# Tying the last batch's butterflies to their written place on VectorE, in a four-layer convolution chain on one Trainium2 core

## The chip, the cores and the metric

The kernel runs on one core of one Trainium2 chip. The metric is the device time of one execution in microseconds. Smaller is better.

## The reference

An input x of shape (4, 64, 256, 256) in 32-bit floats goes through four layers. Layers 0, 1 and 3 are long convolutions along both image axes, with one separable filter per channel, and a residual term. Layer 2 works in a Haar wavelet domain: a two-dimensional transform, two branches that scale, mix the 64 channels and shrink, and the inverse transform with a residual.

```python
# layers 0, 1, 3: k is an outer product of two generated filters per channel
y = jnp.fft.irfft2(u_f * k_f, s=(fft_size, fft_size))[..., :L, :L]
out = y + x * bias[:, None, None]
# layer 2
f1 = haar2d(x)
for i in range(v.shape[0]):
    f3 = f1 * v[i]
    f4 = jnp.einsum('bchw,oc->bohw', f3, conv_w[i])
    f5 = jnp.sign(f4) * jax.nn.relu(jnp.abs(f4) - tau[i])
    acc = acc + f5
y = haar2d(acc, inverse=True)
return y + x
```

## The kernel before, in words

The separable convolutions are matrix products with Toeplitz matrices. One image (a batch entry and a channel, 256 x 256) needs two products per layer: `first` (tile `pa`, copied by ScalarE to a tile `a`) and `second` (tile `py`, to which VectorE adds the residual in L284). Both call `contract`, L253 and L254. PSUM gives all of them four banks in turn (`psm`).

The work of a batch b has three stages. `convolutions` runs layers 0 and 1 and the forward Haar transform. `mixing` runs 64 groups g of layer 2: channel mix on TensorE into `px` (L441), a scaling split between VectorE (L460) and ScalarE (L465), the absolute value and sign on ScalarE, the shrinking on VectorE (L476, L480), and two additions into the large tile `z` (L486). `inverse` then takes 64 channels c, one for each tick: `fetch` copies a channel out of `z` (`zc`, ScalarE, L525), `rows` transforms the rows on TensorE (`pw`, L532 and L533), `join` adds the layer's residual on VectorE (`t` and `u`, L554, L557, L558), and layer 3's two products (`pa`, `py`) and the output follow. For the last batch, b = 3, the stage `mixing` is accompanied by layer 3 of those images of earlier batches that were put off (`convolution`; their input tile is `v`).

The inverse column transform has two forms. The channels 0 to 15 (chunk 0 of `z`) have it done on TensorE: `halves` (`w`, a ScalarE copy in L539 and a VectorE subtraction in L540) and `cols` (`pu`, L546). The channels 16 to 63 (chunks 1, 2 and 3 of `z`) have it done in place by butterflies on VectorE. `level(n, chunk)` calls `halve`, which issues two VectorE instructions on `z`: a subtraction (L291), and an instruction that makes the sum from it (L292), which needs the first one's result. A chunk has levels n = 1, 2, 4, 8 and 16 in one pair each, n = 32 in two pairs and n = 64 in four: eleven pairs, seven of them with 1024 elements for each partition. All pairs of a chunk have to be done before the first channel of the chunk is fetched.

The order of the work is written as a list of events. Every step has a time in ticks, `at(time, run, unit)`, the list is sorted, and the steps are called in that order. In `inverse`, `when` gives a level its tick; for the last batch these are the tick `start + 16 * (chunk - 1)` for n = 1 to 8, the next one for n = 16, and then every second tick for one pair each of n = 32 and n = 64. That list is not yet the order on the engines: a scheduler orders each engine's instructions anew, and an instruction whose inputs it takes to be ready may be issued far ahead of its place in the list. In the program before, the butterflies of the last batch stand where that scheduler put them: chunk 1's levels 1 to 16, and the first steps of chunks 2 and 3, stand within `mixing`, and the rest is spread over the inverse stage's channels 0 to 31.

Of the kernel before, what the change touches and what calls it, by code (L numbers as in the profile page):

```python
# [16 lines left out]
B, C, S, EMB, ORD = 4, 64, 256, 33, 64  # L17
# [8 lines left out]
PLACE = {  # L26
    "load": 0.714,
    "a0": 1.643,
    "a0 copy": 1.643,
    "y0": 2.571,  # L30
    "y0 sum": 2.571,
    "a1": 3.5,
    "a1 copy": 3.5,
    "y1": 4.429,
# [64 lines left out]
def conv_seq_kernel(ctx, tc, x, fz, fw, bias, decay, haar, haar_row, factors, vt, taut, wmix, out):  # L99
# [14 lines left out]
    nc = tc.nc  # L114
# [126 lines left out]
    def toeplitz(layer, c, name):  # L241

        t = tp.tile([P, 2, S], F32, name=name, tag="toep")
        nc.sync.dma_start(t, ap(pads[layer], c * 2 * ROW, [[1, P], [ROW, 2], [1, S]]))
        return t
# [40 lines left out]

        return [product, residual]

    def halve(even, odd):

        nc.vector.tensor_sub(odd, even, odd)  # L291
        nc.vector.scalar_tensor_tensor(even, even, 2.0, odd, ALU.mult, ALU.subtract)  # L292

    def level(n, chunk, begin=0, count=None):

        count = n if count is None else count
        v = z.rearrange("p n s x c -> p n s (x c)")[:, chunk].rearrange("p (j e s) x -> p j e s x", e=2, s=P // 2 // n)
        halve(v[:, begin : begin + count, 0, 0, :], v[:, begin : begin + count, 1, 0, :])

    def butterfly():  # L300

        v = z.rearrange("p n s (h k) c -> p n s h k c", k=2)
        for h in range(2):
            halve(v[:, :, 0, h, 0, :], v[:, :, 0, h, 1, :])
# [6 lines left out]
    def at(time, run, unit):  # L311
        events.append((time, len(events), run, unit))
# [196 lines left out]
    def inverse(b, start, put_off):  # L509

        st = {}

        def early(c):
            r = mx.tile([P, 2, 2, P], F32, name=f"r_{b}_{c}", tag="f", bufs=3)
            nc.sync.dma_start(r, keep[b][c])
            st[c]["r"] = r

        def sooner(c):
            st[c] = {}
            if c not in put_off:  # L520
                st[c][2] = toeplitz(2, c, f"t2_{b}_{c}")

        def fetch(c):
            a = mx.tile([P, 2, 2, P], F32, name=f"zc_{b}_{c}", tag="mag")
            nc.scalar.copy(a.rearrange("p h k i -> p (h k) i"), z[:, c // 16, :, :, c % 16].rearrange("p i x -> p x i"))  # L525
            st[c]["z"] = a

        def rows(c):
            a = st[c]["z"]
            ps = psm.tile([P, 2, 2, P], F32, name=f"pw_{b}_{c}", tag="mm")  # L530
            for m in range(2):
                nc.tensor.matmul(ps[:, 0, m, :], a[:, 0, m, :], hsinv, start=True, stop=True)  # L532
                nc.tensor.transpose(ps[:, 1, m, :], a[:, 1, m, :], ident)  # L533
            st[c]["pw"] = ps

        def halves(c):
            w = st[c]["w"] = mx.tile([P, 2, 2, 2, P], F32R, name=f"w_{b}_{c}", tag="f4")
            ps = st[c]["pw"]
            nc.scalar.copy(w[:, 0], ps)  # L539
            nc.vector.tensor_tensor(w[:, 1], ps, w[:, 0].bitcast(F32), ALU.subtract)  # L540

        def cols(c):
            ps = psm.tile([P, 2, 2, P], F32, name=f"pu_{b}_{c}", tag="mm")
            flat = "p e m w -> p (e m w)"
            for i in range(2):
                nc.tensor.matmul(  # L546
                    ps.rearrange(flat), hb, st[c]["w"][:, i].rearrange(flat), start=(i == 0), stop=(i == 1)
                )
            st[c]["pw"] = ps

        def join(c):
            ps = st[c]["pw"]
            t = io.tile([P, 2, 2, P], F32, name=f"t_{b}_{c}", tag="res", bufs=BUFS["res"])
            nc.vector.scalar_tensor_tensor(t, st[c]["r"], 0.5, ps, ALU.mult, ALU.add)  # L554
            u = io.tile([P, 2, S], F32, name=f"u_{b}_{c}", tag="y", bufs=BUFS["y"])
            v = u.rearrange("p m (w e) -> p m w e", e=2)
            nc.vector.tensor_add(v[:, :, :, 0], t[:, 0], t[:, 1])  # L557
            nc.vector.tensor_sub(v[:, :, :, 1], t[:, 0], t[:, 1])  # L558
            st[c]["u"] = u

        def aside(c):
            nc.scalar.dma_start(late[b, c], st.pop(c)["u"])

        along = start - groups - 3

        def when(tick, n, chunk, *span):
            at(tick + PLACE["level"], lambda _: level(n, chunk, *span), 0)

        at(along + 11 + PLACE["level"], lambda _: butterfly(), 0)
        for chunk in range(1, 4):  # L570
            turn = start + 16 * (chunk - 1)
            for n in (1, 2, 4, 8):
                when(along + 12 + 3 * chunk if b + 1 < B else turn, n, chunk)
            when(turn + 1, 16, chunk)
            for i in range(2):
                when(turn + 2 + 2 * i, 32, chunk, 16 * i, 16)
            for i in range(4):
                when(turn + 6 + 2 * i, 64, chunk, 16 * i, 16)

        for c in range(C):  # L580
            for name, stage in zip(("sooner", "early", "fetch", "rows"), (sooner, early, fetch, rows)):
                at(start + c + PLACE[name], stage, c)
            turn = start + c
            if c < 16:
                at(start + c + PLACE["halves"], halves, c)
                at(start + c + PLACE["cols"], cols, c)
                turn += 1
            at(turn + PLACE["join"], join, c)
            if c in put_off:
                at(turn + PLACE["aside"], aside, c)  # L590
            else:
                for name, stage in zip(("a3", "a3 copy", "y3", "y3 sum", "out"), last(b, st)):
                    at(turn + PLACE[name], stage, c)

    def last(b, st):
        return [
            *first(b, st, "u", 2, "a3"),
            *second(b, st, "a3", 2, "u", "y3", "co"),
            lambda c: nc.scalar.dma_start(out[b, c].rearrange("(k p) w -> p k w", p=P), st.pop(c)["y3"]),
        ]  # L600
# [41 lines left out]
    start = ready + 3  # L642
    for b in range(B):
# [10 lines left out]
        start = max(end + C, ready + 3)  # L654
# [115 lines left out]
```

## Time and profile before

| | |
|---|---|
| median of 3 runs | 2919.81 us (2915.54 to 2923.6) |
| the profiled execution's own time | 2913.15 us |
| its span | 2911.3 us |
| PE busy in the span | 2827.3 us (97%) |
| DVE (VectorE) busy | 2499.0 us (86%) |
| ACT (ScalarE) busy | 2085.2 us (72%) |
| mean granted TensorE clock | 0.997 |

Times within the execution are microseconds from the start of the span. The last batch's `mixing` lies at about 2386 to 2676, its `inverse` at about 2676 to 2911. Busy time of TensorE is modelled at its ends, so a small gap may hide in it. The names PE, DVE and ACT stand for TensorE, VectorE and ScalarE; SP issues the loads.

### The profile page before, as it was taken

Reading aid. Unit: us, or ns where it says so; the run is one execution under the profiler, and the core shown is the slowest. Engines: PE = TensorE matmul, PEld = TensorE weight load, DVE = VectorE, ACT = ScalarE, POOL = GpSimd, SP = SyncE. Lnnn points to the kernel's source line nnn. Section 1 sums busy time; section 2 is a strip of 40 time slices with the busy share of each in tenths; the row PEclk is TensorE's granted clock in tenths of the full one; section 3 lists DMA queues with packets and bytes.
Section 4 is the critical chain, followed back from the end, with each engine's and each line's share of the span. In section 5 each row is a group of like instructions: output and inputs, shape, how many; then the busy total and the mean of one; then the engine's idle time right before and its main releaser. Section 6 shows DMA issues by size and latency. Waiting matters only on the chain. (4 is left out here: it accounts for less than half of the span.)

```text
span 2911.3 us, 52368 instructions
## 1 busy us (share of the span) xinstructions
PE 2827.3 (97%) x16566; PEld 2551.1 (88%) x16566; DVE 2499.0 (86%) x4263; ACT 2085.2 (72%) x4950; POOL 329.7 (11%) x644
## 2 busy tenths in 40 slices
PE   8999999999999999999999899999999899999999
PEld 6899998888888898998898898998898898887898
DVE  4656558999998679999998679999998779999985
ACT  2333338999995558989985558998986568887554
POOL 0111111121120001221211001121211000000000
PEclk9999999999999999999999999999999999999999
DMA  5878777666676886777677886777777888776676
GB/s 162 256 229 233 231 233 222 205 205 206 197 213 205 268 260 198 214 213 212 208 214 237 253 269 195 214 215 212 208 212 233 262 278 233 235 233 199 208 237 208
DMA packets 599367, 649.77 MB, mean 223 GB/s; under 512 B 48465, under 2 KB 517044, under 8 KB 598964
## 3 DMA queue, kind: packets, MB, share of 16 engines
q1 hardware_dynamic: 519860, 562.09, 65.2%
q10 hardware_dynamic: 79232, 84.34, 8.2%
q8 instruction: 134, 2.20, 0.3%
q14 instruction: 141, 1.16, 0.1%
HBM read 426.77 MB, written 219.48 MB: 222 GB/s over the span
## 5 line engine op out<-in xcount | busy, mean ns | idle before, releaser
L253 PE MATMUL py<-t,a 128*128 128x256 f32 x3072 | 920.9, 382 | 7.5 <-ACT a L267 6.9
L267 ACT COPY a<-pa 128x512 f32<-128x512 f32 x768 | 490.7, 639 | 430.3 <-PE pa L254 390.5
L465 ACT ACTIVATE f<-px,vt 128x64 f32<-128x64 f32 x2816 | 620.2, 408 | 95.9 <-DVE f L460 95.6
L254 PEld LDWEIGHTS py<-t,a 128*128 128x128 f32 x3072 | 584.3, 190 | 79.8
L254 PE MATMUL py<-t,a 128*128 128x128 f32 x3072 | 590.8, 274 | 0.0
L253 PEld LDWEIGHTS py<-t,a 128*128 128x128 f32 x3072 | 496.2, 191 | 47.5 <-ACT a L267 16.8
L441 PE MATMUL px<-wb,f 128*128 128x256 f32 x2048 | 490.4, 381 | 11.1 <-ACT f L465 10.6
L441 PEld LDWEIGHTS px<-wb,f 128*128 128x128 f32 x2048 | 367.7, 190 | 56.4 <-ACT f L465 17.6
L525 ACT COPY zc<-z 128x512 f32<-128x512 f32 x256 | 281.5, 1101 | 170.6 <-PE pw L533 143.6
L343 POOL TENSOR_TENSOR sd<-less 128x128 f32<-128x128 f32 (+4 forms) x320 | 189.3, 592 | 1884.7 <-DVE less L342 1616.8
L469 ACT ACTIVATE mag<-f 128x1024 f32<-128x1024 f32 x256 | 304.1, 1188 | 21.0 <-DVE z L486 20.4
L476 DVE TENSOR_TENSOR mag<-mag,vt 128x1024 f32<-128x1024 f32 x256 | 312.4, 1220 | 4.6 <-ACT mag L469 3.4
L480 DVE SCALAR_TENSOR_TENSOR mag<-mag,f 128x1024 f32<-128x1024 f32 x256 | 312.7, 1222 | 1.1 <-DVE mag L476 0.5
L253 PE MATMUL pa<-t,y 128*128 128x256 f32 x1024 | 308.5, 383 | 4.7 <-DVE y L284 2.9
L253 PE MATMUL pa<-t,x 128*128 128x256 f32 x1024 | 305.7, 380 | 0.0
L366 DVE TENSOR_TENSOR sp<-sd,sp 128x512 fp32r<-128x512 f32 x256 | 179.1, 700 | 135.0 <-ACT sp L361 133.8
L472 ACT ACTIVATE f<-f 128x1024 f32<-128x1024 f32 x256 | 291.4, 1138 | 3.2
L253 PE MATMUL pa<-t,u 128*128 128x256 f32 x772 | 236.0, 388 | 39.2 <-issue 18.9
L284 DVE SCALAR_TENSOR_TENSOR y<-u,bsb,py 128x512 f32<-128x512 f32 x193 | 143.9, 745 | 124.6 <-PE py L254 101.3
L284 DVE SCALAR_TENSOR_TENSOR y<-x,bsb,py 128x512 f32<-128x512 f32 x256 | 189.8, 742 | 42.7 <-PE py L254 41.7
L254 PEld LDWEIGHTS pa<-t,y 128*128 128x128 f32 x1024 | 194.7, 190 | 26.5
L254 PEld LDWEIGHTS pa<-t,x 128*128 128x128 f32 x1024 | 194.6, 190 | 26.3
(72 smaller groups left out, 4450.8 us busy)
## 6 DMA issues: line engine op xcount, KB each, us to landing
t<-pad SPq DMA_DIRECT2D x768, 256.0 KB, 4.0
x<-in_x SPq DMA_DIRECT2D x256, 256.0 KB, 3.8
coef<-co SPq DMA_DIRECT2D x256, 256.0 KB, 3.0
f<-coef SPq DMA_DIRECT2D x256, 256.0 KB, 3.1
r<-keep SPq DMA_DIRECT2D x256, 256.0 KB, 3.7
out_y<-y ACTq DMA_DIRECT2D x256, 256.0 KB, 4.0
keep<-sums SPq DMA_DIRECT2D x256, 128.0 KB, 2.8
keep<-sd SPq DMA_DIRECT2D x256, 128.0 KB, 2.8
```

The costliest lines, as they stand in the source:

```text
L253: nc.tensor.matmul(ps[:, m, :], src[:, 0, m * P : (m + 1) * P], t[:, ::-1], start=True, stop=False)
L254: nc.tensor.matmul(ps[:, m, P:], src[:, 1, m * P : (m + 1) * P], t[:, : P - 1 : -1], start=False, stop=True)
L267: nc.scalar.copy(a, s["p" + new])
L284: nc.vector.scalar_tensor_tensor(y, s[res], bsb[:, layer, c : c + 1], s["p" + new], ALU.mult, ALU.add)
L343: engine.tensor_tensor(t[:, :, :, half:length], v[..., 0], v[..., 1], ALU.subtract)
L441: nc.tensor.matmul(ps[:, q, h, :], f[:, q, h * P : (h + 1) * P], wb.rearrange("p r n -> p (r n)"), start=True, stop=True,)
L465: nc.scalar.mul(f4[:, j], px[:, j], scale(g, 0)[:, j : j + 1])
L469: nc.scalar.activation(mag, st[g]["f4"], AF.Abs)
L472: nc.scalar.activation(st[g]["f4"], st[g]["f4"], AF.Sign)
L476: nc.vector.tensor_sub(mag, mag, over(g, 1, 16))
L480: nc.vector.scalar_tensor_tensor(mag, mag, 0.0, st[g]["f4"], ALU.max, ALU.mult)
L525: nc.scalar.copy(a.rearrange("p h k i -> p (h k) i"), z[:, c // 16, :, :, c % 16].rearrange("p i x -> p x i"))
```

## The change

For the last batch, the first instruction of each butterfly pair whose tick lies at or after the start of the inverse stage (these are all 33 pairs of chunks 1 to 3) is given to `tc.keep_in_program_order`. That call adds an edge from the instruction to the one that was called just before it on the same engine. The edge fixes the order of issue and no semaphore is waited for. The second instruction of a pair follows the first by its data. Nothing is computed differently, and no instruction is added or removed.

```diff
-    def halve(even, odd):
-
-        nc.vector.tensor_sub(odd, even, odd)
+    def halve(even, odd, stay=False):
+
+        first = nc.vector.tensor_sub(odd, even, odd)
+        if stay:
+            tc.keep_in_program_order(first)
         nc.vector.scalar_tensor_tensor(even, even, 2.0, odd, ALU.mult, ALU.subtract)
...
-    def level(n, chunk, begin=0, count=None):
+    def level(n, chunk, begin=0, count=None, stay=False):
...
-        halve(v[:, begin : begin + count, 0, 0, :], v[:, begin : begin + count, 1, 0, :])
+        halve(v[:, begin : begin + count, 0, 0, :], v[:, begin : begin + count, 1, 0, :], stay)
...
         def when(tick, n, chunk, *span):
-            at(tick + PLACE["level"], lambda _: level(n, chunk, *span), 0)
+            at(tick + PLACE["level"], lambda _: level(n, chunk, *span, stay=tick >= start and b + 1 == B), 0)
```

In the built program, VectorE's order in the inverse stage becomes the following (`[1]` is the first instruction of a pair, `[2]` the second):

```
channels 3 to 11:  y(k-3) [1] t(k) [2] u(k) u(k) w(k+1)  |  y t w u u  |  y [1] t [2] u u w  |  ...
channels 20 on:    y(k-3) [1] t(k) [2] u(k) u(k)         |  y t u u    |  y [1] t [2] u u    |  ...
at channels 0-2, 15-18 and 32-34: the levels 1 to 16 and the first pair of 32, one after the other between t, u and y
```

The scheduler, which sees the butterflies in other places, also orders a part of the other engines' instructions in this stage anew. One put-off image of layer 3 (its `y` at L284, and its products) moves from before the last `px` to after it; chunk 3's pairs move from channels 18 to 31 to channels 32 to 44.

## The prediction

> **What bounds the kernel now.** I read the busy time by stage first, then VectorE's and TensorE's timelines, then the waits. By stage (columns: stretch, length, busy time of PE, PEld, DVE, ACT, POOL, granted clock, DMA share):
>
> ```profile
> 2410.00:2663.00 253.00, 246.74 (x1333) 218.90 (x1332) 253.00 (x352) 221.50 (x519) 0.00 (x0) 1.00 0.78 232
> 2663.00:2677.00 14.00, 8.33 (x49) 7.16 (x47) 13.95 (x21) 9.99 (x22) 0.00 (x0) 0.96 0.77 227
> 2677.00:2741.00 64.00, 64.00 (x396) 59.00 (x397) 62.85 (x101) 36.64 (x50) 0.00 (x0) 0.96 0.60 189
> 2741.00:2801.00 60.00, 55.45 (x362) 50.97 (x361) 59.33 (x96) 27.51 (x33) 0.00 (x0) 1.00 0.71 216
> 2801.00:2905.00 104.00, 104.00 (x698) 97.45 (x697) 66.54 (x126) 50.40 (x61) 0.00 (x0) 1.00 0.73 225
> ```
>
> In the last batch's mixing VectorE is never idle and TensorE nearly never. At the change of stage TensorE is idle for 5.7 us of 14. In channels 0 to 15 TensorE is full, in 16 to 31 VectorE, and from channel 32 on TensorE alone; there VectorE has 36% to spare. So the butterflies are moved out of a stage that VectorE fills, and partly into one where it has time. Whether they fit depends on how they are bunched, which the timelines tell (columns: start, duration, engine, line, operation; in brackets the idle time before and its releaser):
>
> ```profile
> 2804.78 0.75 DVE L284 SCALAR_TENSOR_TENSOR y<-u,bsb,py 128x512 f32<-128x512 f32 x1 [1.14 <-PE py L254]
> 2805.45 0.69 DVE L554 SCALAR_TENSOR_TENSOR t<-r,pw 128x512 f32<-128x512 f32 x1
> 2806.17 0.43 DVE L557 TENSOR_TENSOR u<-t 128x256 f32<-128x256 f32 x1
> 2806.51 0.42 DVE L558 TENSOR_TENSOR u<-t 128x256 f32<-128x256 f32 x1
> ...
> 2717.49 1.22 DVE L291 TENSOR_TENSOR z<-z 128x1024 f32<-128x1024 f32 x1
> 2718.63 0.74 DVE L284 SCALAR_TENSOR_TENSOR y<-u,bsb,py 128x512 f32<-128x512 f32 x1
> ```
>
> A late tick (channel 32 on) leaves VectorE 1.14 us idle; a large butterfly instruction takes 1.22 and gives way to the next after 1.14. One of them in each tick fits; two don't.
>
> ```profile
> 2676.86 0.80 PE L532 MATMUL pw<-hrow,zc 128*128 128x128 f32 x2 [3.58 <-ACT zc L525]
> ...
> 2749.32 0.70 PE L253 MATMUL pa<-t,u 128*128 128x256 f32 x2 [1.98 <-DVE u L558]
> ...
> 2788.75 0.67 PE L253 MATMUL pa<-t,u 128*128 128x256 f32 x2 [0.26 <-PE pw L533]
> ```
>
> The first is the hole at the change of stage. The others show what late butterflies cost: `pa` waits for `u`. The third is a tick with two large ones, one ahead of `y` and one ahead of `u`: `pw` began at 2787.66 and `pa` follows 0.66 later when nothing is late, so it came 0.43 late, after a `u` that ended at 2788.65 (the bracket's 0.26 counts from the modelled end of `pw`, which it wasn't waiting for).
>
> **What the Trainium skill says.** "TensorE: Matmul & The Clock Gate", What's actually happening: after about 3.4 us without work TensorE runs at half clock until it has been busy for as long. The trace agrees: after the 3.58 us hole `py`'s products took 2.56 us in place of 1.31, for some 6 us. "VectorE: DVE Perf Modes", Mode 1x (REGULAR): one result per cycle for two-tensor 32-bit work, which makes 1.07 us for 1024 elements as an estimate; the trace has 1.22. "Perfetto Trace Analysis", Tensor Engine Instruction: VectorE and ScalarE are strictly first in, first out. So a pinned butterfly stands behind the `y` ahead of it even while that `y` waits; the 1.14 us above are such a wait.
>
> **The change part by part.** No instruction is added or removed. All sums are differences to the profiled execution (2913.15 us; span 2911.3), which lies 6.7 us below the median of the runs.
>
> *Mixing.* Butterfly instructions stand at 2408 to 2631 for 6.5 us (by start-to-start times: 1.87 at 2408, then 0.14, three of 0.34, two of 0.60, and 1.14 twice). From the L460 of group 4 (2410.01) to that of group 63 (2666.87) there are 59 groups of 3.67 (L460 0.73, L476 1.13, L486 0.67, L480 1.14), 54 `y` of 0.66 and 4.62 us of these butterflies: 256.8, as measured. Without them, and with one `y` moved behind, VectorE needs 251.5. But a group with a put-off image takes TensorE 4.35 (1.73 for `px`, 2.62 for the products): 53 x 4.35 + 6 x 3.67 = 252.6, so 4.3 is saved. Of the 1.87 ahead of it only 1.2 can go, since `px` of group 4 ended at 2408.6 and L460 follows 0.2 later. Together -5.5. Bounds: -7.1 (VectorE alone) and -1.2 (TensorE paces all of it).
>
> *Change of stage.* The moved image's 2.62 us fill the hole to about 1 us, so the clock should stay up. Counted from the last addition into `z`, `pu` of channel 3 began after 16.7 us. After the change levels 1 to 16 and a pair of 32 (7.1 us) stand among `w`, `t` and `u` of channels 0 to 2: `w_0` at 3.9, `t_0` at 6.4, `u_0` complete at 9.3 (`pa_0` could start at 7.5), `w_1` at 9.9, `w_2` at 14.05 (`pu_2` could go on at 13.1), and `pu_3` at 17.6. So +0.9: what the clock gives back (2.9) the bunch takes. Bounds -2.2 (no wait for `u` and `w`) and +4 (the clock drops too).
>
> *Pairs in channels 3 to 11* (five, every second tick of 3.74). `y` starts 0.20 after the next `pw` begins (so at 2801.50), at 3.36 of the tick. Then from 4.02: [1] to 5.15, `t` 5.75, [2] 6.88, `u` 7.56, `w` 8.16, and with 0.1 to TensorE 8.26; the second half of `pu` could start at 7.74 (7.48 + 0.26). Each pair stalls TensorE by 0.52: +2.6.
>
> *Channels 15 to 18.* Before, TensorE waited here 1.32, 1.98 and some more: from `pu_15` (2737.20) to `pw_20` (2757.60) 20.4 us. The bunch of chunk 2 (7.1 us, where before some 9 stood) gives 18.9 by the same steps: -1.5.
>
> *Channels 19 to 31.* Per pair: `y` from 0.20 to 0.86, [1] 2.0, `t` 2.6, [2] 3.73, `u` 4.41, `pa` at 4.5; it could start at 3.95. Five pairs of 0.55 are 2.8; before, the stretch lost 1.2 against 3.28 a tick: +1.6.
>
> *Channels 32 to 44*, where before nothing waited: the bunch of chunk 3 stalls `pa_33` by 0.7 and `pa_34` by 2.1, and five pairs cost 0.55 each: +5.6. The last pair ends some 3 ticks before channel 48 is fetched, and the tail from there is as before.
>
> *Queues.* A butterfly issues no transfer. SP's and ScalarE's issues change places by one or two; the DMA engines are busy for 78% in mixing and 60 to 73% after, and no `t` or `y` waited for a load there: nothing, as long as the loads of `r` and `t2` stay a tick ahead. POOL is idle. ScalarE's output issue, which waits for `y`, can hold back `zc` by less than a tick, and `zc` runs two channels ahead.
>
> Sum: -5.5 + 0.9 + 2.6 - 1.5 + 1.6 + 5.6 = +3.7 us.
>
> **The rivals.**
> *(A) A pair costs its whole second butterfly.* Place: `u` to `pa`, and `w` to `pu`, in fifteen ticks; price 1.14 in place of some 0.54, so 15 x 0.6 = 9 more: +12.7. From 0.9 us a pair on the kernel is slower by over 0.3%. For it: VectorE has no slack behind a pinned pair, and a late `u` also delays ScalarE's copy `a`. Against: a double tick cost 0.43 above. The same side is reached if TensorE paces the mixing alone (-1.2): +8.0.
> *(B) The bunches are absorbed.* Over two ticks VectorE's work fits (2 x 2.14 + 2.28 = 6.56 against 6.56). If no pair and no bunch stalls TensorE, all the idle time of before is won: -5.5 - 2.2 - 4.7 (channels 15 to 18) - 1.2 = -13.6. Against: one `psm` turn and the strict order leave about one tick of lead, and TensorE did wait for `u` in the trace.
> *(C) It doesn't do what it says.* The order of the two programs shows all 33 first instructions moved, so this is out; only the second of a pair is free, and its data binds it.
>
> **How the numbers follow.** 0.3% is 8.8 us, about what a measurement of this kernel can tell from no change. Likeliest: gain and loss nearly cancel, +3.7 on 2919.8, so 2923.5 (own range -8 to +8.7). It has 0.54. Rival A with the paced mixing has 0.38, since every term I left out (late copies, late output issues) adds time. Rival B has 0.08. The range goes from -8.8 (2911) to rival A with a little more (2938).
>
> **What would show it.** Right: no L291 and L292 from 2408 to 2670; the first `pw` of channel 0 some 5 us earlier, after a hole of about 1 us and at full clock; `pa` waiting for `u` by about 0.55 in every second tick of channels 20 to 44, and 2 us at channel 34; idle VectorE in the ticks between. Wrong: mixing as long as before; no waits for `u` (B), or waits over 0.9 (A).

## The result, and the profile after

The changed kernel is slower by 0.3 to 0.4%: 2927.36 us (median of 7 runs) against 2915.06 us (7 runs), ratio 1.0038 with a 95% interval of 1.0023 to 1.0052. Measured once more it took 2921.24 us against 2912.42, ratio 1.0030 (1.0018 to 1.0041). Ratios below are always to the kernel before in the same comparison; its own median lies between 2912 and 2920 us in them.

The first profiled execution of the changed kernel took 2927.36 us (span 2925.5), 14.2 us more than that of before. 4.5 us of these were there already when the last batch's mixing began: its first L462 started at 2394.01, where before L460 started at 2389.50. Up to group 4 of that mixing the engines run the same instructions in the same order in both programs, so this part isn't the change's: between 2281 and 2311 that execution had a mean granted clock of 0.95, where before had 1.00, which stands for some 1.5 of the 4.5 us; what the rest comes from stays open. The change itself is judged on the part from the first L462 to the last `y`: 527.65 us after, 517.76 before, so **+9.9 us**.

Below, lines of `kernel.py` behind the edit have moved by two: L460 is L462, L532 is L534, L558 is L560, and L292 is L294. The busy time by stage, for the changed kernel (columns as before: stretch, length, busy time of PE, of PEld, which is TensorE's weight loads, of DVE, ACT and POOL, granted clock, DMA share and GB/s):

```profile
2413.00:2668.00 255.00, 246.18 (x1340) 220.25 (x1339) 253.45 (x348) 225.03 (x529) 0.00 (x0) 1.00 0.79 233
2668.00:2682.00 14.00, 12.07 (x72) 10.46 (x71) 13.18 (x24) 9.69 (x18) 0.00 (x0) 1.00 0.70 195
2682.00:2745.00 63.00, 58.89 (x367) 52.57 (x366) 56.91 (x98) 33.78 (x46) 0.00 (x0) 1.00 0.63 188
2745.00:2809.00 64.00, 58.59 (x371) 53.30 (x370) 52.70 (x90) 27.59 (x33) 0.00 (x0) 0.97 0.70 209
2809.00:2858.00 49.00, 44.04 (x287) 39.92 (x286) 43.68 (x70) 21.93 (x26) 0.00 (x0) 1.00 0.71 210
2858.00:2921.00 63.00, 63.00 (x421) 59.04 (x420) 39.41 (x74) 28.78 (x35) 0.00 (x0) 1.00 0.71 210
```

At the change of stage (second line) TensorE is idle for 1.9 us in place of 5.7, at full clock. In exchange it is idle for 4.1 to 5.4 us in each of the three stretches that hold a chunk's butterflies, also in the one from channel 33 on, where it had been full. Only behind channel 47 is it full again. What it waits for is told by the group of layer 3's first product, in the last batch's part of each execution (columns: line, engine, operation, names, shapes, count, busy us, mean ns, and the idle time before with its releasers). First the kernel before, then the changed one:

```profile
L253 PE MATMUL pa<-t,u 128*128 128x256 f32 x260 | 78.0, 382 | 4.5 <-issue 2.0 <-DVE u L558 2.0 <-PE pw L533 0.5
```
```profile
L253 PE MATMUL pa<-t,u 128*128 128x256 f32 x260 | 78.8, 385 | 12.2 <-DVE u L560 4.8 <-issue 4.7 <-ACT zc L527 1.8
```

The same products wait 7.7 us longer, for `u`. ("issue" and `zc` stand for the same wait: at 2819.30, put down to `zc`, the copy had ended at 2818.67 and `u` at 2819.20; an "issue" is shown next.) How one tick loses its share is seen in the timeline of the changed kernel, here VectorE from the tick that `pw` of channel 38 begins (2829.28):

```profile
2829.48 0.75 DVE L284 SCALAR_TENSOR_TENSOR y<-u,bsb,py 128x512 f32<-128x512 f32 x1 [0.95 <-PE py L254]
2830.14 1.22 DVE L291 TENSOR_TENSOR z<-z 128x1024 f32<-128x1024 f32 x1
2831.28 0.68 DVE L556 SCALAR_TENSOR_TENSOR t<-r,pw 128x512 f32<-128x512 f32 x1
2831.88 1.22 DVE L294 SCALAR_TENSOR_TENSOR z<-z 128x1024 f32<-128x1024 f32 x1
2833.01 0.42 DVE L559 TENSOR_TENSOR u<-t 128x256 f32<-128x256 f32 x1
2833.35 0.41 DVE L560 TENSOR_TENSOR u<-t 128x256 f32<-128x256 f32 x1
```
and TensorE:
```profile
2832.56 0.39 PE L534 MATMUL pw<-hrow,zc 128*128 128x128 f32 x2
...
2833.86 0.67 PE L253 MATMUL pa<-t,u 128*128 128x256 f32 x2 [0.47 <-issue]
2834.37 0.38 PE L254 MATMUL pa<-t,u 128*128 128x128 f32 x2
```

`pw` began at 2832.56, and `pa` follows it 0.66 later when nothing is late, so at 2833.22. The second butterfly stands ahead of `u`, `u` ends at 2833.76, and `pa` begins at 2833.86: 0.64 late. Its first two products then take 0.51 in place of 0.43. So the tick has 4.00 us in place of 3.285. A tick like this, with both instructions of a large pair ahead of one `u`, is called a double tick below; it costs **0.71 us**. In channels 3 to 11 the same cost is 0.61 (ticks of 4.35 in place of 3.745). A chunk's levels 1 to 16 with its first pair of 32, which follow one after the other, are called its bunch.

### The profile page after: what moved, and what is told of

Its sections match the earlier page's. It is cut to its first block, busy times and chain, and to the rows that moved or that the text cites. A ratio compares the mean times of both kernels' runs of the same rounds, so it can differ in the third digit from the quotient of the medians.

```text
span 2925.5 us, 52366 instructions
## 1 busy us (share of the span) xinstructions
PE 2830.4 (97%) x16566; PEld 2552.2 (87%) x16566; DVE 2500.5 (85%) x4263; ACT 2086.9 (71%) x4950; POOL 330.1 (11%) x644
## 5 line engine op out<-in xcount | busy, mean ns | idle before, releaser
L467 ACT ACTIVATE f<-px,vt 128x64 f32<-128x64 f32 x2816 | 622.8, 406 | 94.8 <-DVE f L462 94.0
L482 DVE SCALAR_TENSOR_TENSOR mag<-mag,f 128x1024 f32<-128x1024 f32 x256 | 312.7, 1222 | 1.1 <-DVE mag L478 0.5
L284 DVE SCALAR_TENSOR_TENSOR y<-u,bsb,py 128x512 f32<-128x512 f32 x193 | 143.7, 744 | 134.1 <-PE py L254 109.1
L284 DVE SCALAR_TENSOR_TENSOR y<-x,bsb,py 128x512 f32<-128x512 f32 x256 | 189.5, 740 | 43.4 <-PE py L254 43.2
```

The source lines that it names most:

```text
L284: nc.vector.scalar_tensor_tensor(y, s[res], bsb[:, layer, c : c + 1], s["p" + new], ALU.mult, ALU.add)
L467: nc.scalar.mul(f4[:, j], px[:, j], scale(g, 0)[:, j : j + 1])
L482: nc.vector.scalar_tensor_tensor(mag, mag, 0.0, st[g]["f4"], ALU.max, ALU.mult)
```

## The experiments

Everything is read from the same landmarks: the first and last L462 of the last batch's mixing, the first `pw` of channels 5, 15, 20, 33 and 47, and the last `y`. Each number is how much longer that part took than in the profiled execution of the kernel before, in us. The last two columns are the sum over these parts and the measured ratio of all runs.

| kernel | mixing | to channel 5 | 5 to 15 | 15 to 20 | 20 to 33 | 33 to end | sum | ratio (95%) |
|---|---|---|---|---|---|---|---|---|
| predicted | -5.5 | +0.9 | +2.6 | -1.5 | +1.6 | +5.6 | +3.7 | 1.0013 |
| changed | -3.7 | +0.9 | +3.0 | +0.5 | +2.6 | +6.6 | +9.9 | 1.0038 (1.0023 to 1.0052) |
| again | -3.4 | +0.9 | +3.0 | -1.2 | +2.6 | +6.6 | +8.5 | 1.0030 (1.0018 to 1.0041) |
| behind_u | -3.6 | +0.9 | 0.0 | -2.2 | -1.0 | +3.1 | -2.8 | 0.9988 (0.9982 to 0.9995) |
| one_per_tick | -3.4 | 0.0 | 0.0 | -1.2 | -1.0 | +2.6 | -2.9 | 0.9990 (0.9984 to 0.9996) |
| spread_small | -3.7 | +1.0 | +3.0 | -2.6 | +3.7 | +5.0 | +6.4 | 1.0022 (1.0014 to 1.0031) |
| both | -3.5 | +0.9 | 0.0 | -3.5 | +0.6 | 0.0 | -5.5 | 0.9977 (0.9968 to 0.9987) |
| spread_all | -3.7 | -1.8 | 0.0 | -2.3 | -0.9 | 0.0 | -8.6 | 0.9967 (0.9956 to 0.9978) |
| no_butterflies | -3.6 | -2.0 | 0.0 | -3.5 | -1.0 | 0.0 | -10.1 | 0.9968 (0.9956 to 0.9980) |
| chunks_1_2 | 0.0 | +1.5 | +5.0 | +1.6 | +2.6 | 0.0 | +10.7 | 1.0042 (1.0029 to 1.0054) |
| ticks_untied | 0.0 | 0.0 | 0.0 | -0.9 | +0.2 | 0.0 | -0.8 | 0.9997 (0.9989 to 1.0005) |

The theory under test is **placement**: what counts is how many large butterflies stand ahead of a `u` on VectorE, not that they were moved into this stage. Its rivals are **amount** (VectorE hasn't the time for them here, wherever they stand) and **clock** (the loss is half clock after TensorE's holes). A fourth, that the loss comes from another order on TensorE or ScalarE, is out for five of these kernels: in again, behind_u, one_per_tick, spread_small and both, these two engines run the same instructions in the same order as in the changed kernel, so that VectorE's order alone makes the difference.

**again**: the changed kernel unaltered.

> The changed kernel unaltered, to see which of its parts repeat. Placement theory (the order of the butterflies sets the cost): from the first L462 of the last batch's mixing to the last y the execution takes about 10 us more than in the kernel before (+9.9 in the first pair of profiles: mixing -3.7, channels 0 to 4 +0.9, channels 5 to 14 +3.0, channels 17 to 20 +0.5, channels 20 to 33 +2.6, channels 33 to 47 +6.6), and a double tick costs 0.6 (channels 3 to 11) and 0.7 us (later), each time the same. Clock theory (a good part of the loss is a half clock after the holes): the half clock at channels 18 and 19 recurs, and the sum varies with it by 2 us. The 3.4 us that the first profile lost at 2230 to 2390, where both programs are identical, come back only if they belong to the program; chance theory: they are gone or elsewhere. Time 2923 to 2930.

Every part repeats within 0.4 us but one, channels 15 to 20. There the first execution had 1.7 us more, and the profile shows why. The changed kernel, first execution, TensorE in the tick of channel 18:

```profile
2753.85 0.70 PE L253 MATMUL pa<-t,u 128*128 128x256 f32 x2 [1.98 <-DVE u L560]
...
2755.42 1.06 PE L253 MATMUL py<-t,a 128*128 128x256 f32 x2
2756.27 0.64 PE L254 MATMUL py<-t,a 128*128 128x128 f32 x2
```
and the same tick in the repetition:
```profile
2751.21 0.70 PE L253 MATMUL pa<-t,u 128*128 128x256 f32 x2 [1.98 <-DVE u L560]
...
2752.62 0.60 PE L253 MATMUL py<-t,a 128*128 128x256 f32 x2
```

After the same hole of 1.98 us the products took 1.06 (half clock) once and 0.60 once. The tick had 8.50 us with it and 6.84 without. So the clock is worth 1.7 us of 9.9 in one execution and nothing in the other; it isn't the main cause. The 4.5 us ahead of the mixing were 1.5 us here, and between -1.2 and +6.2 in the other kernels, all of which have the same order up to that point: chance.

**behind_u**: the pairs of 32 and 64 behind `u`.

```diff
-            at(tick + PLACE["level"], lambda _: level(..., stay=tick >= start and b + 1 == B), 0)
+            tied = tick >= start and b + 1 == B
+            behind = 0.53 if tied and n >= 32 else PLACE["level"]
+            at(tick + behind, lambda _: level(n, chunk, *span, stay=tied), 0)
```

> The pairs of n = 32 and 64 are written behind u and w of their tick rather than ahead of t, still tied; the first of a pair then stands between u and the next y, the second between that y and the next t, one large butterfly for each tick. Placement theory: fifteen double ticks cost nothing any more, so 3.0 + 3.6 + 3.6 = 10.2 us less than the changed kernel: about 2917, ratio to the kernel before about 1.001. The rival, amount (VectorE has too little time in this stage for the butterflies that left the mixing, wherever they stand): no gain, about 2927, ratio 1.004. Clock theory (the loss is mainly half clock after the holes of the bunches): the bunches stay, so about 2926.

All fifteen double ticks vanish. Against again 11.3 us are won, 10.1 for them and 1.0 in the tick of channel 18, and the kernel is faster than before. VectorE's timeline in this kernel, around `pw` of channel 40 (2820.53):

```profile
2819.51 1.22 DVE L291 TENSOR_TENSOR z<-z 128x1024 f32<-128x1024 f32 x1
2820.73 0.75 DVE L284 SCALAR_TENSOR_TENSOR y<-u,bsb,py 128x512 f32<-128x512 f32 x1
2821.40 1.22 DVE L294 SCALAR_TENSOR_TENSOR z<-z 128x1024 f32<-128x1024 f32 x1
2822.53 0.68 DVE L556 SCALAR_TENSOR_TENSOR t<-r,pw 128x512 f32<-128x512 f32 x1
2823.24 0.43 DVE L559 TENSOR_TENSOR u<-t 128x256 f32<-128x256 f32 x1
2823.59 0.42 DVE L560 TENSOR_TENSOR u<-t 128x256 f32<-128x256 f32 x1
2824.01 0.75 DVE L284 SCALAR_TENSOR_TENSOR y<-u,bsb,py 128x512 f32<-128x512 f32 x1
```

The same instructions fill VectorE with hardly a gap, and TensorE's ticks are 3.28 and 3.29. Only one butterfly stands between a `y` and its `u`; the other fits in the time in which VectorE would have waited for `py`. Amount is refuted: not one instruction fewer is in this stage.

**one_per_tick**: is it the place behind `u`, or that there is one for each tick?

```diff
+            if tied and n >= 32:
+                at(tick + PLACE["level"], lambda _: level(n, chunk, *span, stay=True, part=0), 0)
+                at(tick + 1 + PLACE["level"], lambda _: level(n, chunk, *span, stay=True, part=1), 0)
+                return
```

> The two instructions of each pair of n = 32 and 64 are written in successive ticks, each tied, and both ahead of t (not behind u): y [1] t u u | y [2] t u u. The bunches stay as in the changed kernel. Placement theory, by number: one large butterfly of 1.13 ahead of t makes u late by 1.13 against 1.8 of slack, so the fifteen pairs cost nothing: the stage 11 us under the changed kernel, as in behind_u, at about -2.8, ratio 0.999. Rival, by position: only what stands behind u is free, whatever stands ahead of t holds up u and pa; then each large butterfly costs about half of a double tick, 0.35, and the stage stays near +8, ratio 1.003.

The double ticks are gone here as well, with both instructions ahead of `t`. So it is the number. One large butterfly makes `u` 1.13 later, and a `u` with nothing in its way is complete more than that ahead of its `pa`: in the kernel before, the `u` that ended at 2806.93 had its `pa` at 2808.53. Two butterflies, 2.27, are more than these 1.6.

**spread_small** and **both**: the bunches.

```diff
-            for n in (1, 2, 4, 8):
-                when(along + 12 + 3 * chunk if b + 1 < B else turn, n, chunk)
+            later = b + 1 == B and chunk > 1
+            for n, ticks in ((1, 3), (2, 3), (4, 2), (8, 1)):
+                when(along + 12 + 3 * chunk if b + 1 < B else turn - ticks * later, n, chunk)
             when(turn + 1, 16, chunk)
...
-                when(turn + 2 + 2 * i, 32, chunk, 16 * i, 16)
+                when(turn + 2 + later + 2 * i, 32, chunk, 16 * i, 16)
```

(and the same `later` for n = 64).

> The bunches of chunks 2 and 3 are spread: n = 1 and 2 three ticks ahead of their turn, n = 4 two ahead, n = 8 one ahead, the pairs of 32 and 64 one tick later; the pairs stand ahead of t as in the changed kernel. Placement theory: chunk 3's bunch (3.05 us at channels 34 and 35) goes, but its seven large pairs now each cost 0.71, so channels 33 to 47 take 1.2 less; chunk 2's bunch goes from 5.2 us over full pace (3.0 of holes and 2.1 of half clock) to about 1.3, and one pair more at 0.7 is paid: 3.2 less. Together about 4.4 less than the changed kernel: 2923, ratio 1.0025, and no half clock at channels 18 and 19. Amount: 2927. Clock theory: only the 2.1 us of the half clock go: 2925.

> Both edits: bunches of chunks 2 and 3 spread, and all tied pairs of n = 32 and 64, and all of chunks 2 and 3, written behind u. Placement theory: -10.2 for the pairs, -3.05 for chunk 3's bunch, -3.9 for chunk 2's: 17 us less than the changed kernel, about 2910, ratio to the kernel before 0.998, so faster than both. Amount: 2927, ratio 1.004, with idle TensorE wherever VectorE is full. Clock theory: about 2925.

Both ratios came as the placement theory had them (1.0022 for 1.0025, and 0.9977 for 0.998). In spread_small chunk 3's bunch goes, but two more double ticks take its place, and channels 20 to 33 have one more, six in all, the last of them with small levels of chunk 3 in it. In both, chunk 3's bunch and pairs cost nothing (ticks of 3.28 and 3.29 from channel 31 on). The profiled executions of both and of the changed kernel differ by 15.4 us in the sum, where 17 were expected; what is missing is a new loss of 1.5 us in the tick of channel 20, where a butterfly and two `y` stand ahead of one `u`.

**chunks_1_2**: chunk 3 not tied (`and chunk < 3` in the condition).

> Undoes one part: chunk 3 is not tied, chunks 1 and 2 are tied as in the changed kernel. In the built order chunk 3's first five pairs' instructions stand in the mixing again (n = 1 to 16) and the rest between channels 0 and 18. Placement theory: channels 33 to 47 run at full pace (+6.6 gone); about 3 us come back in the mixing (groups with a butterfly of 0.6 or 1.1 us take longer than the 3.85 of those without an image), and channels 3 to 14, where the odd ticks now hold one large instruction too, and channels 15 to 19 lose 1 to 3 more: the stage about +6 to +7.5 in place of +8.5, ratio 1.0022. Amount: chunk 3's 19 us of VectorE are paid in full in stages that VectorE fills: +20 or more.

Channels 33 to 47 run at full pace, as expected, and yet the sum is worse than again, 3 us over the expectation. The mixing gave back all of its gain. The double ticks of channels 3 to 11 cost 1.0 each in place of 0.61, since the ticks between them now hold a large butterfly too. And a hole of 3.52 us opens at channel 18, with half clock behind it. Undoing the most expensive part of the change does not help, since its work has to stand somewhere; that it costs 2 us more there and not 20 is again placement, not amount.

**spread_all**: a list of ticks for each chunk, every pair tied and at 0.53, behind `u`.

```diff
+TICKS = (
+    (0, 0, 1, 2, 3, 5, 7, 9, 11, 13, 15),
+    (14, 14, 16, 17, 18, 20, 22, 24, 26, 28, 30),
+    (29, 29, 31, 32, 34, 36, 38, 40, 42, 44, 46),
+)
...
+            for tick, n in zip(ticks, (1, 2, 4, 8, 16)):
+                when(start + tick, n, chunk)
```

(and `ticks[5:]` for the pairs of 32 and 64).

> All three chunks by a list of ticks, every pair tied behind u: chunk 1 at ticks 0, 0, 1, 2 (n = 1, 2, 4, 8), 3 (16), 5, 7 (32), 9 to 15 (64); chunk 2 at 14, 14, 16, 17, 18, 20, 22, 24 to 30; chunk 3 at 29, 29, 31, 32, 34, 36, 38, 40 to 46. Against the kernel called both, chunk 1's bunch at channels 0 to 2 is spread as well. Placement theory: TensorE's holes of 1.8, 0.7 and 0.5 us at channels 2 and 3 close (2 us won), and channels 17 to 21 lose less: from -5.5 us in the stage (both) to about -8, ratio to the kernel before 0.9968. Amount: VectorE is full in channels 0 to 15 (chunk 1 alone has 19 us and the stage leaves it about 1.2 in each tick of 3.74), so what is won at channels 2 and 3 is lost again up to channel 15: -5.5, ratio 0.9977.

**no_butterflies**: the floor.

> Leaves out all eleven pairs of chunks 1, 2 and 3 of the last batch, so the inverse column transform of its channels 16 to 63 is missing: the floor, what all butterflies cost together wherever they stand. Placement theory: mixing -3.6 as in the changed kernel; in the inverse stage TensorE is full from channel 4 on: channels 17 to 22 take 5 ticks of 3.285 and one image of 2.62 more, 19.0 us (23.8 before, 21.8 in both), channels 22 to 33 take 36.1 (37.1 before); with 1 to 3 us less at channels 0 to 5 the stage stands at -11, ratio 0.9963. Amount: if butterflies in the inverse stage cost VectorE's time wherever they stand, the floor lies far below the kernel called both: -15 or less.

The two have the same ratio, 0.9967 and 0.9968; in the profiled executions 1.5 us lie between them. The floor came at -10.1 where placement had -11 and amount -15 or less. The group of `pa`'s products, in spread_all and in no_butterflies:

```profile
L258 PE MATMUL pa<-t,u 128*128 128x256 f32 x260 | 77.9, 382 | 1.3 <-DVE u L565 1.0 <-PE pa L259 0.3
```
```profile
L253 PE MATMUL pa<-t,u 128*128 128x256 f32 x260 | 77.6, 380 | 1.0 <-ACT a L267 1.0
```

12.2 us of waiting have become 1.3, with all butterflies in the inverse stage: they cost almost nothing where they stand one for each tick. spread_all beats both kernels: 2907.95 us against 2918.39 on its chip.

**ticks_untied**: the same list without the tie (`tied = False`).

> The list of ticks of spread_all without any tie. In the built order the scheduler takes the first steps of all three chunks back into the mixing (ten small instructions at group 4, two of 256 elements, two of 512 and two of 1024 further on), three large ones stand at the change of stage, chunk 2's bunch at channels 15 to 19 and chunk 3's pairs at 20 to 32, much as in the kernel before. Placement theory (the order on VectorE decides, and the tie is what fixes it): mixing about 0 against the kernel before, the half clock at channel 0 back, the stage at -1 to +2, ratio 1.000. Rival (the later ticks alone make the gain, the tie adds nothing): -8.6, ratio 0.997.

As expected, it takes as long as the kernel before. The scheduler takes the small levels back into the mixing, whose gain is gone but for 0.04 us, and the first tick of the inverse stage is 4.00 again. TensorE's whole order is that of the kernel before. The list alone is worth nothing that can be measured; the tie is what makes it hold.

## Why the prediction was right, and where it was off

The time lay in the range, 2911 to 2938, and the mechanism was that of the likeliest case: a gain in the mixing, a hole that is filled, and `u` late in fifteen ticks and three bunches; what paces the mixing afterwards was not read rightly. But the sum was +3.7 where +9.9 and +8.5 were measured in the profiles. With that the result stands at the line between "within 0.3%" (0.54) and "slower by more" (0.38). Nearly every term came out slower than predicted, and none faster to make up for it. That the time itself lies nearer (2923.5 predicted, 2927.4 measured) than the difference is luck: the prediction counted from 2919.8, the median of three runs, and over seven runs the kernel before stands at 2915.06. These are the terms:

- **Mixing**, -5.5 predicted, -3.4 to -3.7 in every kernel without butterflies in it. The 1.2 ahead of group 4 were right (20.51 became 19.32). The failing step is "53 x 4.35 + 6 x 3.67 = 252.6" for groups 4 to 63, which took 254.3. 43 of these 59 groups took 4.333 each, and in them both engines are full: VectorE's own steps make 4.33. The other 16 lost time behind L482, whose next instruction the sum had start 1.14 after it. In eight of them L462 stands directly behind L482 and starts 0.17 to 0.19 later than that (1.4 us together), so that the five groups without a `y` took 3.85 in place of 3.67; in eight more another instruction starts 0.10 to 0.12 later (0.9), five times a `y` that waits for `py`. These are 2.3 of the 2.8 us by which the stretch exceeds the 251.5 of VectorE alone. One of the first eight:

```profile
2507.46 1.21 DVE L482 SCALAR_TENSOR_TENSOR mag<-mag,f 128x1024 f32<-128x1024 f32 x1
2508.78 0.82 DVE L462 TENSOR_TENSOR f<-px,vt 128x640 f32<-128x640 f32 x1
```

  L462 starts 1.32 after L482 did, which is 0.11 after its end at 2508.67. The kernel keeps two tiles `f4` (`f` in the profile) in turn, and the one that this L462 writes is the one that L482 reads; in the trace's semaphore records it is L482 that releases it. So VectorE waits for the end of its own instruction. In the kernel before, no group from 4 to 62 has this: a `y`, an addition or a butterfly stands between L480 and the next L460. The butterflies had covered a wait there, and taking them out won less than their time. (TensorE waits in this group as well, 1.48 us for ScalarE's L467, but the `px` that it then begins at 2507.23 is the one for the L462 at 2513.12, not for this one.) This is read from the traces; no run took the wait away, nor was the `y` that left the mixing with its image (0.66) told apart from the butterflies. In the sum for the kernel before, two slips cancel: groups 4 to 62 have 55 `y` and 58 pairs of L486, not 54 and 59.
- **Change of stage**, +0.9 predicted, +0.9 measured: from the last addition into `z` (it gives way to the next instruction at 2676.37) to `pu` of channel 3 (2693.99) there are 17.6 us, as worked out, and the clock stays up (1.00). The hole at `pw` was not 1 us but nothing. `pa` of channel 0 waited 1.79 for `u`, where the bunch stands, as in the working (9.3 against 7.5). spread_all and no_butterflies show what the bunch costs: 2.7 and 3.0 us.
- **Pairs in channels 3 to 11**, +2.6 predicted, +3.0 measured: 0.61 each in place of 0.52.
- **Channels 15 to 18**, -1.5 predicted, -1.2 in the repetition: right in size. In the first execution +0.5, by the half clock that the prediction had looked for at the change of stage only.
- **Channels 19 to 31**, +1.6 predicted, +2.6 measured; **channels 32 to 44**, +5.6 predicted, +6.6 measured. The bunch was nearly right (1.0 and 2.05 us in two ticks, predicted 0.7 and 2.1). The term that was too small is the pair: 0.55 predicted, 0.71 measured, ten times: 1.6 of the 2.0 us. The steps up to the second butterfly fit to 0.01 us (0.20, 0.86, 2.00, 2.60, 3.73). What was mis-sized is the end: the last `u` lasts 0.41 while the sum took the 0.34 by which it gives way to the next, and the first two products after a wait take 0.08 more, which was left out. TensorE's start 0.10 after the `u` was in the sum.

Of the signs, "no L291 and L292 from 2408 to 2670" was met but for one pair of 64 elements at 2412, which belongs to `butterfly` and isn't tied. The first `pw` of channel 0 came 3.7 us earlier, counted from the first L462, where 5 were expected. The idle time of VectorE in the ticks between is there (0.95). Rival A's sums (+8.0, +12.7) enclose what was measured, but not its mechanism: no pair of the changed kernel cost 1.14 or even 0.9, and the mixing gained three times 1.2. Rival B (all absorbed) fell, and behind_u shows that its own reckoning was right (two ticks hold the work) and its order was not: the work fits when it is one butterfly for each tick, and a pair ahead of one `u` doesn't.

## What to carry to other kernels

On an engine that works in order, count filler work for each deadline, not for the stage: one piece of 1.13 us ahead of `u` cost nothing, two cost 0.71 us, though the idle time of two ticks was enough for both. A tie that only fixes the order is worth what the written order is worth: with the same tie the kernel was 0.3% slower, 0.1% faster or 0.3% faster than before, and without it the best list gained nothing. Before taking the time of filler work that leaves an engine as a gain, look at what it had covered: L462 directly behind L482 starts 1.32 us after it in place of 1.14, since it waits for its end. To find such a wait, add up an in-order engine by the steps between starts, and take the full duration wherever something needs the end, on another engine or on the same.

## What was not expected of the hardware

Half clock came after a hole of 1.98 us. Five executions have that very hole at channel 18 (the kernel before, the changed one, again, one_per_tick and ticks_untied), and one of them lost 1.7 us by it. The traces' records of the granted clock tell which. In each execution the stretches of half clock begin at multiples of 3.413 us from one another (in the first one of the changed kernel at 765.1, 908.5, 1621.8, 2280.6 and 2755.1), and each lasts one or two such periods. In that execution the hole, from 2751.87 to 2753.85, lay whole in the period from 2751.66 to 2755.07; TensorE was idle for 58% of it, and the next period ran at half clock. In the other four a border between two periods cut the hole in two, and neither period was idle for more than 51%. In all eleven traces, from 25 us on, each of the 47 drops follows a period in which TensorE was idle for at least 54%, by its modelled ends, and no period without a drop behind it was idle for more than 56%.

The Trainium skill, "TensorE: Matmul & The Clock Gate", What's actually happening, has the clock fall after an idle window of about 3.4 us, and says that the window runs freely, not with the work. The periods agree with the second. On the first the measurement differs, and it decides here: a window idle for little more than its half was enough. So a hole of 2 us can cost 1.7 us more than its own length or nothing, by where it falls among the windows, and that differs from one execution to the next.
